# A new opening for a fused graph layer and attention kernel

## The chip, the cores and the metric

The kernel runs on one core of one Trainium2 chip. The metric is the device time of one execution in microseconds; a kernel's time is the median of its runs.

## The reference, cut to what matters

x has 64 elements of 256 nodes by 512 channels (float32), adj is one 256 by 256 graph. Two layers follow each other, both with a residual and a normalization over the channels:

```python
# layer 0
mi = x @ Wi.T;  mj = x @ Wj.T            # W = [Wi, Wj], each 512 x 512
x = layernorm(x + deg[:, None] * (mi + b) + adj @ mj)
# layer 1: masked attention with 8 heads of 64
q, k, v = x @ Wq.T + bq, x @ Wk.T + bk, x @ Wv.T + bv
x = layernorm(x + softmax(mask(q k^T / 8)) v @ Wo.T + bo)
```

## The kernel before, in words

Elements are worked on in 32 groups of two. A tile of x or h has 128 partitions, two row tiles t (nodes) or four column tiles c (channels). The work is written out by hand: nearly every instruction goes through `in_order`, which keeps an engine's instructions in the order of the program text, and the text interleaves the stages of several elements. What isn't passed to `in_order` (in the kernel before, the loads of weights, biases and graph and the stores of factors) is placed by a scheduler.

**Layer 0** (`l0_steps`) computes mi and mj of one element in full fp32 with seven products of blocks instead of eight: sums S1 to S4 of blocks of the transposed x (`sum_x`, `left_steps`) meet combinations T1 to T4 of blocks of the weights. `w0` holds the seven right-hand sides, B11, B21, B22, T1 to T4 (`combine` subtracts one from another). A product is two matmuls of 128x128 by 128x512. Results are put together on VectorE: `u1`, `u2`, `u3` are partial sums, `add_scaled` adds a degree-scaled one to the residual tile `xh`, `mj` is written to SBUF and split into `hi` and `lo`, two fp32r parts that TensorE multiplies at four times the fp32 pace. `neighbours` multiplies both by the graph; `add`, `stat`, `give` finish the layer (residual, statistics with the power on GpSimd, normalization on ScalarE). Before that, `add_bias` on GpSimd adds the degree-scaled bias `degb` to `xh`.

The transposed x comes from `xB`, loaded by `load_xB` in four transfers into one single buffer and turned on VectorE by `turn_x`. `xh` is loaded apart by `load_x`.

**Layer 1** computes q, k, v and the output with three fp32r products each. Left and right sides are split in three parts: `hA`, `hL`, `hD` for h (`split_three`), and head, lift and diff for the weights: one "factor" is a quarter of one of four weight matrices. A step of v, q or k is twelve matmuls. In the first group each of the sixteen factors is made on the chip from the raw weights (`make`) and stored to DRAM (`kept`); later groups load them from there. `bring` fetches or makes the next factor of `queue` into a ring of six buffers (`stream`) and appends it to `coming`, from which the steps (`v_step`, `qk_step`) take theirs.

PSUM has three pools: `ps_m` with three banks (tag mm), `ps_s` with two pairs of banks (tag sc, for scores and some products) and one bank `ps_v`.

**The opening** is the text between the definition of `combine` and the loop over groups: layer 0 of elements 0 and 1, the split of h by transposes on TensorE (`h_transpose`), six factors made at once, then v, q and k of group 0, with the first products of element 2 between k and the scores. All later groups run in the loop.

```python
    run([p[0], p[2], p[3]])
    turn_x(1, "kT")
    ...
    run([p[1], p[4], p[5], q[0], p[6], low0, q[2]])
```

Of the kernel before, what the change touches and what calls it, by code (L numbers as in the profile page):

```python
# [224 lines left out]
def unshifted_path(ctx, tc, flag, x, adj, wiT, wjT, b0, wqT, bq, wkT, bk, wvT, bv, woT, bo, out):  # L225
# [49 lines left out]
    def score_bank(name):  # L275
        return score_banks(name)[:, 0, :]
# [5 lines left out]
    def in_order(ins):  # L282

        tc.keep_in_program_order(ins)
# [7 lines left out]
    def transpose(*args):  # L292
        in_order(nc.tensor.transpose(*args))
# [19 lines left out]
    load_xB(0)  # L313
    w0 = const.tile([P, 7, 2, D], F32, name="w0")
    adj_i = p2.tile([P, NT, N], I32, tag="pe", name="adj_i")
    for n, w, h in ((B11, wiT, 0), (T3, wjT, 0), (None, None, 0), (B21, wiT, 1), (B22, wjT, 1)):
        if n is None:
            nc.sync.dma_start(out=adj_i, in_=adj.rearrange("(t p) j -> p t j", p=P))
        else:
            nc.sync.dma_start(out=w0[:, n], in_=w.rearrange("(p h c) o -> p h c o", h=2, c=2)[:, h])  # L320
    load_x(0)
    nc.sync.dma_start(out=b_bc, in_=b0.to_broadcast([P, D]))

    xT, xS, hP, qT, kT, vv, aoT, aoP = ({} for _ in range(8))

# [21 lines left out]
        in_order(nc.vector.tensor_reduce(deg, a, AX.X, ALU.add))  # L347

    def turn_graph():
        for t in range(NT):  # L350
            pt = score_bank("pt_a")[:, :N]
            for i in range(NT):
                transpose(pt[:, i * P:(i + 1) * P], a[:, i, t * P:(t + 1) * P], ident)

            in_order(nc.vector.tensor_copy(graph[:, t, :], pt))
            in_order(nc.scalar.copy(aT[:, t, :], pt))

    inexact = const.tile([P, 1], F32, name="inexact")

# [7 lines left out]

    def degree_bias():
        for t in range(NT):
            in_order(nc.vector.tensor_scalar(degb[:, t, :], b_bc, deg[:, t:t + 1], None, ALU.mult))  # L370

    def add_bias(b):
        in_order(nc.gpsimd.tensor_tensor(xh[b], xh[b], degb, ALU.add))  # L373
# [1 line left out]

    def load_bias(b, name):
        t = const.tile([P, NC], F32, tag=name, name=name)
        nc.sync.dma_start(out=t, in_=b)
        return t

    def channels(q):

        half, j = divmod(q, 2)
        return slice(j * DH + half * R, j * DH + (half + 1) * R)

    def load_wo(t, c0):
        w = woT.rearrange("(c p) o -> p c o", p=P)
        for q in range(P // R):
            nc.sync.dma_start(out=t[q * R:(q + 1) * R], in_=w[channels(q), c0:c0 + t.shape[1], :])

    bq_sb = load_bias(bq, "bq")
    bk_sb = load_bias(bk, "bk")

    bv_t = const.tile([P, NC], F32, tag="bvt", name="bv_t")
    with nc.allow_non_contiguous_dma(reason="512 numbers, once"):
        for q in range(P // R):
            nc.sync.dma_start(out=bv_t[q * R:(q + 1) * R], in_=bv.rearrange("r (c p) -> p (r c)", p=P)[channels(q)])
    bo_bc = const.tile([P, D], F32, name="bo_bc")
    nc.sync.dma_start(out=bo_bc, in_=bo.to_broadcast([P, D]))
# [6 lines left out]
    def load_raw(name, tiles):  # L406
        n = NC // len(tiles)
        for i, t in enumerate(tiles):
            if name == "wo":
                load_wo(t, n * i)  # L410
            else:
                w = weights[name].rearrange("(p c) o -> p c o", p=P)
                nc.sync.dma_start(out=t, in_=w[:, n * i:n * (i + 1), :])
        raws[name] = tiles

    def raw_tile(tag):
# [14 lines left out]
    queue = []  # L431
    coming = []

    def bring():
        if queue:
            name, j, first = queue.pop(0)
            f = stream.tile([P, 3, D], F32R, tag="factor", name="factor")
            if first:
                make(f, name, j)
            else:  # L440
                in_order(nc.scalar.dma_start(out=f.bitcast(F32), in_=kept[name][j]))
            coming.append(f)

    def make(f, name, j):
        head, lift, diff = (f[:, i, :].rearrange("p (c o) -> p c o", c=NC) for i in range(3))
        low = p3.tile([P, NC, P], F32, tag="lu", name="low")
        for cs, raw in pieces(name, j):
            in_order(nc.scalar.activation(head[:, cs], raw, AF.Identity, scale=DOWN))
            in_order(nc.vector.tensor_sub(low[:, cs], raw, head[:, cs].bitcast(F32)))
            in_order(nc.scalar.activation(lift[:, cs], low[:, cs], AF.Identity, scale=LIFT))  # L450
        in_order(nc.vector.scalar_tensor_tensor(diff, low, LIFT, head.bitcast(F32), ALU.mult, ALU.subtract))
        nc.sync.dma_start(out=kept[name][j], in_=f.bitcast(F32))

    def fold_value_bias():

# [56 lines left out]
    def l0_steps(b):  # L512
# [75 lines left out]
        def give(t):  # L588
# [3 lines left out]
        return ([step1, step2, step3, step4, step5, step6, step7], neighbours, add, stat, give,  # L592
                lambda: lows(0))

    def three(tags):
        return [p1.tile([P, NC, NB * N], F32R, tag=t, name=t) for t in tags]

# [102 lines left out]
    def v_evict(g, i, t, banks):  # L700
        X, Y = banks
        dst = vv[g][:, i, t, :]
        in_order(nc.scalar.activation(dst, X, AF.Identity, scale=UP))
        in_order(nc.vector.tensor_add(dst, Y, dst))

    def v_step(g, i, t, kind, last):
        def run():
            if g not in vv:
                vv[g] = p1.tile([P, NB, NT, D], F32, tag="v", name="v_sb")
            banks = pair(kind)  # L710
            for c in range(NC):
                rows_of_product(banks, hP[g], NT * i + t, coming[0 if last else c], c)
                if last:
                    coming.pop(0)
                    bring()
            v_evict(g, i, t, banks)
        return run

    def v_pair(g, i, kinds, last):
# [238 lines left out]
    combine(T1, T3, B11)  # L958
    degrees()
    combine(T2, B22, T1)  # L960
    combine(T4, B21, T2)
    combine(T3, B22, T3)
    (p, nb0, add0, stat0, give0, low0), (q, nb1, add1, stat1, give1, low1) = l0_steps(0), l0_steps(1)
    run([p[0], p[2], p[3]])
    turn_x(1, "kT")
    load_xB(2)
    degree_bias()
    add_bias(0)
    turn_graph()
    run([p[1], p[4], p[5], q[0], p[6], low0, q[2]])  # L970
    add_bias(1)
    sum_x(1)
    run([q[1], nb0])
    for t in (1, 0):
        add0(t)
        stat0(t)
    give0(1)
    run(q[3:4])
    give0(0)
    h_transpose(0, 1)  # L980
    run(q[4:6])
    h_transpose(0, 0)
    run(q[6:7])
    low1()
    for _ in range(RING):
        bring()
    spread_value_bias()
    v, q_, k = projection_steps(0, "SMSM", False)
    run([v[0], nb1])
    for t in (1, 0):  # L990
        add1(t)
        stat1(t)
    v[1]()
    give1(1)
    h_transpose(1, 1)
    give1(0)
    run(v[3:4])
    h_transpose(1, 0)
    run(v[2:3])
    check_graph()  # L1000
    load_raw("wo", [p1.tile([P, NT, D], F32, tag=t, name="raw") for t in ("mj", "hi")])
    for m in range(NC):
        q_[m]()
        if m < NC - 1:
            k[m]()
        if m == 1:
            turn_x(2)
            load_xB(3)
            add_bias(2)
    load_x(3)  # L1010
    p, q = layer0(1)
    run(p[0][:3])
    sum_x(2)
    turn_x(3)
# [216 lines left out]
```

## Time and profile before

| | us |
|---|---|
| median of 3 runs | 3016.53 (3013.96 to 3017.73) |
| profiled execution, whole | 3014.01 |
| its span, first to last instruction | 3012.2 |
| granted TensorE clock, mean over the span | 0.994 |
| TensorE busy | 2936.1 (97%) |
| VectorE busy | 2327.9 (77%) |
| first matmul of layer 0 starts | 9.31 |
| first scores start | 115.72 |
| a group in the loop | about 93 to 94 |

The profile is of one execution. In its rows an engine is PE (TensorE), PEld (its weight loads), DVE (VectorE), ACT (ScalarE), POOL (GpSimd) or SP (the queue that issues most transfers); L290 is the helper through which all matmuls go, so rows are told apart by the tiles that they write and read (`po<-w,xT`). A name in brackets with an arrow is what ended an engine's idle time before the row. The factors' ring is `factor`; `pxy`, `px` and `py` are the banks of v, q and k.

### The profile page before, as it was taken

How to read it: one execution, taken by the hardware profiler on the slowest of the kernel's cores; microseconds unless marked ns; L12 is line 12 of the kernel's file. 1: busy time of each engine (PE TensorE's matmuls, PEld its weight loads, DVE VectorE, ACT ScalarE, POOL GpSimd, SP SyncE). 2: the span in 40 equal slices, each digit the busy share in tenths (PEclk: the TensorE clock that was granted, in tenths of full speed). 3: DMA queues.
4: the chain of work that ended last, by engine and by line, in shares of the span. 5: the costliest groups of instructions: out<-in, count | busy, mean ns of one | idle time of the engine just before them, and what ended most of it. 6: DMA issues, size and time to landing. Idle time of an engine off the chain costs nothing. (4 is left out here: it accounts for less than half of the span.)

```text
span 3012.2 us, 42600 instructions
## 1 busy us (share of the span) xinstructions
PE 2936.1 (97%) x15638; PEld 1915.1 (64%) x15638; DVE 2327.9 (77%) x3539; ACT 1196.1 (40%) x2247; POOL 1247.8 (41%) x930
## 2 busy tenths in 40 slices
PE   6999999999999999999999999999999999999998
PEld 3566666666666666666666666666666666666655
DVE  6778877778777788776788777887777887777875
ACT  2344344343343343443434443433434434334343
POOL 1144443443443444444444434444344444344443
PEclk8999999999999999999999999999999999999999
DMA  5475556674566655566655566655566555666553
GB/s 197 161 246 190 171 189 229 232 247 148 179 209 230 242 208 170 189 219 226 233 164 191 196 234 238 219 172 182 206 232 238 185 171 198 233 234 216 166 172 133
DMA packets 305605, 609.49 MB, mean 202 GB/s; under 512 B 27632, under 2 KB 189424, under 8 KB 305136
## 3 DMA queue, kind: packets, MB, share of 16 engines
q10 hardware_dynamic: 75808, 391.02, 34.0%
q1 hardware_dynamic: 229584, 215.69, 24.7%
q8 instruction: 126, 2.06, 0.3%
q14 instruction: 87, 0.71, 0.1%
HBM read 494.67 MB, written 78.64 MB: 190 GB/s over the span
## 5 line engine op out<-in xcount | busy, mean ns | idle before, releaser
L831 POOL TENSOR_TENSOR pk<-pe 128x512 f32<-128x512 f32 x256 | 330.5, 1301 | 572.5 <-ACT pe L821 572.5
L290 PE MATMUL po<-w,xS 128*128 128x512 f32 x1024 | 481.7, 603 | 3.5 <-DVE mj L560 2.5
L290 PE MATMUL po<-w,xT 128*128 128x512 f32 x768 | 373.8, 610 | 15.3 <-DVE xS L490 9.3
L472 POOL TENSOR_TENSOR rstd<-ve,mhalf 128x1 f32<-128x1 f32 x256 | 154.1, 602 | 512.5 <-DVE below L470 512.4
L821 ACT ACTIVATE pe<-pe 128x1024 f32<-128x1024 f32 x256 | 270.6, 1057 | 151.7 <-DVE pe L817 151.7
L290 PEld LDWEIGHTS po<-w,xS 128*128 128x128 f32 x1024 | 184.0, 189 | 224.5 <-issue 168.2
L608 POOL TENSOR_TENSOR hL<-hF,hA 128x512 fp32r<-128x512 f32 x93 | 150.9, 1622 | 396.6 <-ACT hA L602 396.6
L817 DVE TENSOR_TENSOR pe<-ps,maskT 128x1024 f32<-128x1024 f32 x256 | 300.9, 1196 | 3.6 <-PE ps L290 3.6
L697 DVE TENSOR_TENSOR kT<-py,kT 128x512 f32<-128x512 f32 x128 | 88.5, 691 | 260.2 <-ACT kT L695 260.2
L373 POOL TENSOR_TENSOR xh<-xh,degb 128x1024 f32<-128x1024 f32 x64 | 152.5, 2382 | 271.8 <-DMA xh<-in_x_dram 107.7
L290 PEld LDWEIGHTS po<-w,xT 128*128 128x128 f32 x768 | 139.1, 191 | 189.5 <-issue 171.7
L290 PE MATMUL ps<-qT,kT 64*128 64x256 f32 x2048 | 256.5, 389 | 0.0
L290 PE MATMUL pav<-pe,v_sb 128*32 128x256 f32 x4096 | 248.7, 382 | 3.5 <-DVE kT L697 1.5
L290 PEld LDWEIGHTS ps<-qT,kT 64*128 64x128 f32 x2048 | 187.0, 186 | 69.3 <-PE pav L290 38.7
L908 DVE RECIPROCAL rden<-den 128x256 f32<-128x256 f32 x127 | 221.9, 1747 | 5.6 <-PE den L290 3.8
L477 ACT ACTIVATE shift<-below,rstd 128x1 f32<-128x1 f32 x256 | 74.4, 291 | 374.0 <-POOL rstd L472 223.3
L290 PEld LDWEIGHTS pav<-pe,v_sb 128*32 128x32 f32 x4096 | 118.4, 109 | 155.2 <-issue 49.2
L478 ACT ACTIVATE xh<-xh,shift,rstd 128x512 f32<-128x512 f32 x256 | 208.8, 816 | 8.8
L859 POOL TENSOR_TENSOR aoT<-aoT,spread 128x512 f32<-128x512 f32 x127 | 205.8, 1621 | 3.4 <-DMA spread<-rden 3.0
L602 ACT ACTIVATE hA<-hF 128x512 fp32r<-128x512 f32 x124 | 77.8, 628 | 296.1 <-DVE hF L496 266.5
L290 PE MATMUL px<-hA,factor 128*128 128x512 f32 x640 | 184.3, 410 | 0.0
L290 PE MATMUL py<-hD,factor 128*128 128x512 f32 x640 | 175.4, 396 | 2.1 <-ACT kT L695 2.1
(133 smaller groups left out, 6053.9 us busy)
## 6 DMA issues: line engine op xcount, KB each, us to landing
factor<-wv ACTq DMA_DIRECT2D x124, 768.0 KB, 6.3
factor<-wq ACTq DMA_DIRECT2D x124, 768.0 KB, 6.6
factor<-wk ACTq DMA_DIRECT2D x124, 768.0 KB, 6.3
factor<-wo ACTq DMA_DIRECT2D x120, 768.0 KB, 7.3
xB<-in_x_dram SPq DMA_DIRECT2D x256, 128.0 KB, 3.5
xh<-in_x_dram SPq DMA_DIRECT2D x64, 512.0 KB, 9.0
h_cols<-xh SPq DMA_DIRECT2D x124, 256.0 KB, 2.3
hB<-h_cols SPq DMA_DIRECT2D x124, 256.0 KB, 3.2
```

Of the source, the lines that this page charges most:

```text
L290: in_order(nc.tensor.matmul(*args, **kw))
L373: in_order(nc.gpsimd.tensor_tensor(xh[b], xh[b], degb, ALU.add))
L472: order(nc.gpsimd.tensor_tensor(rstd, ve, mhalf, ALU.pow))
L478: order(nc.scalar.activation(t, t, AF.Identity, bias=shift, scale=rstd))
L602: in_order(nc.scalar.activation(parts[0], src, AF.Identity, scale=DOWN))
L608: in_order(engine.tensor_tensor(parts[1], src, parts[0].bitcast(F32), ALU.subtract))
L697: in_order(nc.vector.tensor_add(dst, Y, dst))
L817: in_order(nc.vector.tensor_add(pe.rearrange("p j t q -> p j (t q)"), ps.rearrange("p j t q -> p j (t q)"), maskT.rearrange("p t q -> p (t ...
L821: in_order(nc.scalar.activation(flat, flat, AF.Exp, scale=QSCALE, accum_out=etot[:, NB * g + i, pr:pr + 1]))
L831: in_order(nc.gpsimd.tensor_tensor(pk, pe[:, :, 0, :], pe[:, :, 1, :], ALU.add))
L859: in_order(nc.gpsimd.tensor_tensor(d, d, spread, ALU.mult))
L908: in_order(nc.vector.reciprocal(rden, den))
```

## The change

Only the opening and the order of loads are rewritten.

- Layer 0 of elements 0 and 1 uses the new `direct_steps`: eight matmuls for mi and eight for mj, each of 128x128 by 128x512, added up in PSUM. No sums of x and none of the partial sums on VectorE are needed. `mj` stays in PSUM and is split from there. Element 2 and all later ones keep `l0_steps`.
- Three products of element 2 move from behind k to between the steps of v.
- `make` is cut in `begin_make` (head on ScalarE, low on GpSimd instead of VectorE) and `end_makes` (lift on ScalarE, diff on VectorE, store), so several factors can be begun before the first is finished. The first four lows get buffers of their own, in the space of qT; later ones alternate between two (tag hF).
- All loads and stores of the opening go through `in_order`, in a new order: weights of mj before those of mi, the graph and the bias next, the raw weights and later x behind; small loads last.
- The degree bias and the copies of the turned graph move from VectorE to ScalarE.
- Before the first product, 24 matmuls of `ones` by `ones` (128x128 by 128x128) run into the bank of `ps_v`.
- In `qk_step`, also within the loop, `bring` stands after VectorE's addition instead of before it.

The diff, cut to its core:

```diff
-    for n, w, h in ((B11, wiT, 0), (T3, wjT, 0), (None, None, 0), (B21, wiT, 1), (B22, wjT, 1)):
-        if n is None:
-            nc.sync.dma_start(out=adj_i, ...
-    load_x(0)
-    nc.sync.dma_start(out=b_bc, in_=b0.to_broadcast([P, D]))
+    for n, w, h in ((T3, wjT, 0), (B22, wjT, 1), (B11, wiT, 0), (B21, wiT, 1)):
+        in_order(nc.sync.dma_start(out=w0[:, n], ...
...
     def turn_graph():
+        both = score_banks("pt_a")
...
-            in_order(nc.vector.tensor_copy(graph[:, t, :], pt))
-            in_order(nc.scalar.copy(aT[:, t, :], pt))
+        in_order(nc.scalar.copy(graph, both[:, :, :N]))
+        in_order(nc.scalar.copy(aT, both[:, :, :N]))
...
-            in_order(nc.vector.tensor_scalar(degb[:, t, :], b_bc, deg[:, t:t + 1], None, ALU.mult))
+            in_order(nc.scalar.activation(degb[:, t, :], b_bc, AF.Identity, scale=deg[:, t:t + 1]))
...
+    def bring(several=1, left=1):
+        for _ in range(several):
+            if queue:
+                name, j, first = queue.pop(0)
+                f = stream.tile([P, 3, D], F32R, tag="factor", name="factor")
+                coming.append(f)
+                if first:
+                    begin_make(f, name, j)
+                    end_makes(left)
+                else:
+                    end_makes()
+                    in_order(nc.scalar.dma_start(out=f.bitcast(F32), in_=kept[name][j]))
...
+    def begin_make(f, name, j):
+        head, lift, diff = cut(f)
+        low = lows.pop() if lows else p2.tile([P, NC, P], F32, tag="hF", name="low")
         for cs, raw in pieces(name, j):
             in_order(nc.scalar.activation(head[:, cs], raw, AF.Identity, scale=DOWN))
-            in_order(nc.vector.tensor_sub(low[:, cs], raw, head[:, cs].bitcast(F32)))
-            in_order(nc.scalar.activation(lift[:, cs], low[:, cs], AF.Identity, scale=LIFT))
-        in_order(nc.vector.scalar_tensor_tensor(diff, low, LIFT, head.bitcast(F32), ALU.mult, ALU.subtract))
-        nc.sync.dma_start(out=kept[name][j], in_=f.bitcast(F32))
+        for cs, raw in pieces(name, j):
+            in_order(nc.gpsimd.tensor_tensor(low[:, cs], raw, head[:, cs].bitcast(F32), ALU.subtract))
+        started.append((f, low, name, j))
+
+    def end_makes(left=0):
+        while len(started) > left:
+            f, low, name, j = started.pop(0)
+            head, lift, diff = cut(f)
+            in_order(nc.scalar.activation(lift, low, AF.Identity, scale=LIFT))
+            in_order(nc.vector.scalar_tensor_tensor(diff, low, LIFT, head.bitcast(F32), ALU.mult, ALU.subtract))
+            in_order(nc.sync.dma_start(out=kept[name][j], in_=f.bitcast(F32)))
...
+    def direct_steps(b):
...
+        def graph_half(h):
+            if h == 0:
+                k["mj"] = score_banks("po")
+            for t in (1, 0):
+                for c in range(2):
+                    matmul(k["mj"][:, t, :], left(t, h)[:, c, :], w0[:, (T3, B22)[h], c, :],
+                           start=(h == 0 and c == 0), stop=(h == 1 and c == 1))
+
+        def own_half(t):
+            k["mi", t] = bank("po")
+            for h in range(2):
+                for c in range(2):
+                    matmul(k["mi", t], left(t, h)[:, c, :], w0[:, (B11, B21)[h], c, :], ...
+
+        def halves(t):
...
+            in_order(nc.scalar.copy(k["hi"][:, t, :], k["mj"][:, t, :]))
+            in_order(nc.vector.tensor_tensor(k["lo"][:, t, :], k["mj"][:, t, :], k["hi"][:, t, :].bitcast(F32),
+                                             ALU.subtract))
+
+        def add_own(t):
+            r = xh[b][:, t, :]
+            in_order(nc.vector.scalar_tensor_tensor(r, k["mi", t], deg[:, t:t + 1], r, ALU.mult, ALU.add))
...
             in_order(nc.scalar.activation(dst, X, AF.Identity, bias=bias[:, m:m + 1], scale=UP))
+            in_order(nc.vector.tensor_add(dst, Y, dst))
             bring()
-            in_order(nc.vector.tensor_add(dst, Y, dst))
...
+    warm = value_bank("warm")
+    for _ in range(24):
+        matmul(warm[:, :P], ones, ones, start=True, stop=True)
+    in_order(nc.sync.dma_start(out=adj_i, in_=adj.rearrange("(t p) j -> p t j", p=P)))
+    in_order(nc.sync.dma_start(out=b_bc, in_=b0.to_broadcast([P, D])))
     turn_x(0)
+    load_x(0)
     load_xB(1)
     load_x(1)
-    load_x(2)
     load_raw("wv", raw_tile("v"))
+    load_xB(2)
     load_raw("wq", raw_tile("aoT"))
     load_raw("wk", [p5.tile([P, NT, D], F32, tag="xh", name="raw") for _ in range(2)])
-    sum_x(0)
...
+    load_x(2)
+    bq_sb, bk_sb = small_loads()
...
+    mj0(0)
+    mj0(1)
+    halves0(1)
+    halves0(0)
     degrees()
+    mi0(1)
+    turn_graph()
     degree_bias()
     add_bias(0)
     add_bias(1)
+    combine(T1, T3, B11)
+    turn_x(1, "kT")
+    own0(1)
+    mi0(0)
+    nb0()
+    combine(T2, B22, T1)
+    own0(0)
+    add0(1)
+    stat0(1)
     give0(1)
+    add0(0)
+    stat0(0)
     give0(0)
+    combine(T4, B21, T2)
+    mj1(0)
+    mj1(1)
+    bring(3, 9)
+    turn_x(2, "xT")
+    load_xB(3)
+    halves1(1)
+    halves1(0)
+    bring(1, 9)
+    mi1(1)
+    own1(1)
     h_transpose(0, 1)
+    mi1(0)
+    own1(0)
     h_transpose(0, 0)
+    nb1()
+    load_raw("wo", ...
+    end_makes()
+    add_bias(2)
...
+    add1(1)
+    stat1(1)
+    give1(1)
+    add1(0)
+    stat1(0)
+    give1(0)
     v[1]()
+    p[0][0]()
+    v[0]()
+    p[0][2]()
     h_transpose(1, 1)
+    h_transpose(1, 0)
+    p[0][1]()
     run(v[3:4])
+    bring(2)
+    end_makes()
+    combine(T3, B22, T3)
     run(v[2:3])
```

In the last v step, `v_step` calls `bring(2, 9)` once its second column is done and `bring(2)` after its eviction. q and k then alternate, as before, with `sum_x(2)`, `check_graph` and `spread_value_bias` among them; `turn_x(3)` and `load_x(3)` follow, then the first scores.

More of the change, by code (lines that the diff above doesn't have):

```diff
@@ L315, in unshifted_path @@
     adj_i = p2.tile([P, NT, N], I32, tag="pe", name="adj_i")
-    for n, w, h in ((B11, wiT, 0), (T3, wjT, 0), (None, None, 0), (B21, wiT, 1), (B22, wjT, 1)):
-        if n is None:
-            nc.sync.dma_start(out=adj_i, in_=adj.rearrange("(t p) j -> p t j", p=P))
-        else:
-            nc.sync.dma_start(out=w0[:, n], in_=w.rearrange("(p h c) o -> p h c o", h=2, c=2)[:, h])
-    load_x(0)
-    nc.sync.dma_start(out=b_bc, in_=b0.to_broadcast([P, D]))
+    for n, w, h in ((T3, wjT, 0), (B22, wjT, 1), (B11, wiT, 0), (B21, wiT, 1)):
+        in_order(nc.sync.dma_start(out=w0[:, n], in_=w.rearrange("(p h c) o -> p h c o", h=2, c=2)[:, h]))
     xT, xS, hP, qT, kT, vv, aoT, aoP = ({} for _ in range(8))
@@ L349, in turn_graph @@
     def turn_graph():
+        both = score_banks("pt_a")
         for t in range(NT):
-            pt = score_bank("pt_a")[:, :N]
             for i in range(NT):
-                transpose(pt[:, i * P:(i + 1) * P], a[:, i, t * P:(t + 1) * P], ident)
-            in_order(nc.vector.tensor_copy(graph[:, t, :], pt))
-            in_order(nc.scalar.copy(aT[:, t, :], pt))
+                transpose(both[:, t, i * P:(i + 1) * P], a[:, i, t * P:(t + 1) * P], ident)
+        in_order(nc.scalar.copy(graph, both[:, :, :N]))
+        in_order(nc.scalar.copy(aT, both[:, :, :N]))
     inexact = const.tile([P, 1], F32, name="inexact")
@@ L377, in load_bias @@
         t = const.tile([P, NC], F32, tag=name, name=name)
-        nc.sync.dma_start(out=t, in_=b)
+        in_order(nc.sync.dma_start(out=t, in_=b))
         return t
@@ L388, in load_wo, with small_loads @@
         for q in range(P // R):
-            nc.sync.dma_start(out=t[q * R:(q + 1) * R], in_=w[channels(q), c0:c0 + t.shape[1], :])
-    bq_sb = load_bias(bq, "bq")
-    bk_sb = load_bias(bk, "bk")
+            in_order(nc.sync.dma_start(out=t[q * R:(q + 1) * R], in_=w[channels(q), c0:c0 + t.shape[1], :]))
+    def small_loads():
+        with nc.allow_non_contiguous_dma(reason="512 numbers, once"):
+            for q in range(P // R):
+                in_order(nc.sync.dma_start(out=bv_t[q * R:(q + 1) * R],
+                                           in_=bv.rearrange("r (c p) -> p (r c)", p=P)[channels(q)]))
+        in_order(nc.sync.dma_start(out=bo_bc, in_=bo.to_broadcast([P, D])))
+        return load_bias(bq, "bq"), load_bias(bk, "bk")
     bv_t = const.tile([P, NC], F32, tag="bvt", name="bv_t")
-    with nc.allow_non_contiguous_dma(reason="512 numbers, once"):
-        for q in range(P // R):
-            nc.sync.dma_start(out=bv_t[q * R:(q + 1) * R], in_=bv.rearrange("r (c p) -> p (r c)", p=P)[channels(q)])
     bo_bc = const.tile([P, D], F32, name="bo_bc")
-    nc.sync.dma_start(out=bo_bc, in_=bo.to_broadcast([P, D]))
     weights = {"wq": wqT, "wk": wkT, "wv": wvT, "wo": woT}
@@ L412, in load_raw @@
                 w = weights[name].rearrange("(p c) o -> p c o", p=P)
-                nc.sync.dma_start(out=t, in_=w[:, n * i:n * (i + 1), :])
+                in_order(nc.sync.dma_start(out=t, in_=w[:, n * i:n * (i + 1), :]))
         raws[name] = tiles
@@ L432, in unshifted_path @@
     coming = []
[L434 to L446, printed above, removed]
+    started, lows = [], []
@@ L447, in make, with cut @@
+    def cut(f):
+        return [f[:, i, :].rearrange("p (c o) -> p c o", c=NC) for i in range(3)]
+    def begin_make(f, name, j):
+        head, lift, diff = cut(f)
+        low = lows.pop() if lows else p2.tile([P, NC, P], F32, tag="hF", name="low")
         for cs, raw in pieces(name, j):
             in_order(nc.scalar.activation(head[:, cs], raw, AF.Identity, scale=DOWN))
-            in_order(nc.vector.tensor_sub(low[:, cs], raw, head[:, cs].bitcast(F32)))
-            in_order(nc.scalar.activation(lift[:, cs], low[:, cs], AF.Identity, scale=LIFT))
@@ L593, in l0_steps, with left, neighbours, add @@
                 lambda: lows(0))
+    def direct_steps(b):
+        k = {}
+        stats = {}
+        def left(t, h):
+            return xT[b][:, 2 * h:2 * h + 2, t * P:(t + 1) * P]
+        def graph_half(h):
[9 more added lines that the diff above has]
+                for c in range(2):
+                    matmul(k["mi", t], left(t, h)[:, c, :], w0[:, (B11, B21)[h], c, :], start=(h == 0 and c == 0),
+                           stop=(h == 1 and c == 1))
+        def halves(t):
+            if t == 1:
+                k["hi"] = p1.tile([P, NT, D], F32R, tag="hi", name="hi")
+                k["lo"] = p1.tile([P, NT, D], F32R, tag="lo", name="lo")
+            in_order(nc.scalar.copy(k["hi"][:, t, :], k["mj"][:, t, :]))
[4 more added lines that the diff above has]
+            in_order(nc.vector.scalar_tensor_tensor(r, k["mi", t], deg[:, t:t + 1], r, ALU.mult, ALU.add))
+        def neighbours():
+            k["pa"] = score_banks("pa")
+            for n, (part, j) in enumerate((part, j) for part in ("hi", "lo") for j in (1, 0)):
+                for i in (1, 0):
+                    matmul(k["pa"][:, i, :], graph[:, j, i * P:(i + 1) * P], k[part][:, j, :],
+                           start=(n == 0), stop=(n == 2 * NT - 1))
+        def add(t):
+            r = xh[b][:, t, :]
+            in_order(nc.vector.tensor_add(r, k["pa"][:, t, :], r))
+        def stat(t):
+            stats[t] = norm_stats(xh[b][:, t, :], in_order)
+        def give(t):
+            norm_apply(xh[b][:, t, :], *stats[t], in_order)
+        return graph_half, own_half, halves, add_own, neighbours, add, stat, give
     def three(tags):
@@ L714, in run @@
                     coming.pop(0)
-                    bring()
+                    if c == 1:
+                        bring(2, 9)
             v_evict(g, i, t, banks)
+            if last:
+                bring(2)
         return run
@@ L956, in unshifted_path @@
     load_raw("wk", [p5.tile([P, NT, D], F32, tag="xh", name="raw") for _ in range(2)])
-    sum_x(0)
-    combine(T1, T3, B11)
-    degrees()
[L960 to L966, printed above, removed]
+    load_x(2)
+    bq_sb, bk_sb = small_loads()
+    mj0, mi0, halves0, own0, nb0, add0, stat0, give0 = direct_steps(0)
@@ L967, in unshifted_path @@
+    mj1, mi1, halves1, own1, nb1, add1, stat1, give1 = direct_steps(1)
+    spare_lows = p1.tile([P, NC, NC, P], F32, tag="qT", name="lows")
+    lows.extend(spare_lows[:, c] for c in range(NC))
+    mj0(0)
+    mj0(1)
+    halves0(1)
+    halves0(0)
+    degrees()
+    mi0(1)
+    turn_graph()
     degree_bias()
     add_bias(0)
-    turn_graph()
-    run([p[1], p[4], p[5], q[0], p[6], low0, q[2]])
     add_bias(1)
[L972 to L976, printed above, removed]
+    combine(T1, T3, B11)
@@ L977, in unshifted_path @@
+    turn_x(1, "kT")
[6 more added lines that the diff above has]
+    stat0(1)
     give0(1)
-    run(q[3:4])
+    add0(0)
+    stat0(0)
     give0(0)
+    combine(T4, B21, T2)
[9 more added lines that the diff above has]
+    own1(1)
     h_transpose(0, 1)
-    run(q[4:6])
+    mi1(0)
+    own1(0)
     h_transpose(0, 0)
[L983 to L986, printed above, removed]
@@ L987, in unshifted_path @@
-    spread_value_bias()
-    v, q_, k = projection_steps(0, "SMSM", False)
[L989 to L992, printed above, removed]
+    nb1()
+    load_raw("wo", [p1.tile([P, NT, D], F32, tag=t, name="raw") for t in ("mj", "hi")])
+    end_makes()
+    add_bias(2)
+    v, q_, k = projection_steps(0, "SMSM", False)
+    p, q = layer0(1)
+    add1(1)
[4 more added lines that the diff above has]
+    give1(0)
     v[1]()
-    give1(1)
+    p[0][0]()
+    v[0]()
+    p[0][2]()
@@ L995, in unshifted_path @@
     h_transpose(1, 1)
-    give1(0)
+    h_transpose(1, 0)
+    p[0][1]()
     run(v[3:4])
-    h_transpose(1, 0)
+    bring(2)
+    end_makes()
+    combine(T3, B22, T3)
     run(v[2:3])
-    check_graph()
-    load_raw("wo", [p1.tile([P, NT, D], F32, tag=t, name="raw") for t in ("mj", "hi")])
     for m in range(NC):
         q_[m]()
+        if m == 1:
+            sum_x(2)
+        if m == 2:
+            check_graph()
+            spread_value_bias()
         if m < NC - 1:
             k[m]()
[L1006 to L1009, printed above, removed]
+    turn_x(3)
@@ L1010, in unshifted_path @@
     load_x(3)
[L1011 to L1014, printed above, removed]
     run([scores(0, 0), scores(0, 1), p[0][3], k[NC - 1]])
```

## The prediction

> **What bounds the kernel now.** I read the page's shares first, then stretches of the opening, then PE's order of time there.
>
> ```profile
> PE 2936.1 (97%) x15638; PEld 1915.1 (64%) x15638; DVE 2327.9 (77%) x3539; ACT 1196.1 (40%) x2247; POOL 1247.8 (41%) x930
> ...
> PE   6999999999999999999999999999999999999998
> ```
>
> PE is the bound, and its only slack is the first slice (75 us). The steady loop leaves nothing to gain (its groups last 93 to 94 us at 99 to 100% PE), and the change leaves it alone but for one move. So the question is when the loop's work can start. The stretches show it (us; then busy us and instructions of each engine, granted clock, DMA share, GB/s):
>
> ```profile
> 0.00:9.31 9.31, 0.00 (x0) 0.03 (x1) 3.26 (x5) 1.28 (x1) 0.88 (x8) 1.00 0.61 167
> 9.31:28.77 19.46, 12.98 (x28) 5.17 (x29) 11.69 (x16) 1.29 (x3) 2.34 (x1) 1.00 0.85 295
> 28.77:54.90 26.13, 19.28 (x48) 8.97 (x48) 19.13 (x33) 6.78 (x12) 3.61 (x3) 0.93 0.26 72
> 54.90:66.59 11.69, 9.66 (x21) 5.92 (x21) 8.45 (x15) 6.89 (x14) 0.00 (x0) 0.58 0.85 338
> 66.59:83.17 16.58, 12.72 (x46) 9.01 (x44) 9.26 (x21) 5.66 (x11) 3.42 (x3) 0.89 0.37 103
> 83.17:109.52 26.35, 21.69 (x85) 16.89 (x84) 20.94 (x33) 15.37 (x32) 0.00 (x0) 0.90 0.67 261
> 109.52:115.72 6.20, 6.20 (x14) 2.50 (x13) 1.44 (x2) 1.27 (x2) 0.00 (x0) 0.86 1.01 358
> 115.72:134.37 18.65, 18.65 (x62) 9.63 (x61) 13.58 (x15) 3.96 (x7) 9.91 (x5) 1.00 0.40 139
> ```
>
> From 109.52 PE never pauses again. I take the first scores (115.72) as the mark: everything after it is the same in both kernels. Between 9.31 and 115.72 PE is idle for 23.9 us (106.41 less the busy 82.5).
>
> Prices on PE (start, us, what; one fp32 matmul leaves two records, an fp32r one a single record):
>
> ```profile
> 9.31 3.45 PE L290 MATMUL po<-w,xT 128*128 128x512 f32 x4 [9.31 <-DVE xS L490]
> ...
> 20.38 3.60 PE L290 MATMUL po<-w,xS 128*128 128x512 f32 x8
> ...
> 58.33 0.80 PE L290 MATMUL pxy<-factor,hD 128*128 128x512 f32 x1 [0.48 <-DVE factor L451]
> ...
> 83.17 1.07 PE L290 MATMUL pxy<-hA,factor 128*128 128x512 f32 x4
> 84.08 1.07 PE L290 MATMUL pxy<-hD,factor 128*128 128x512 f32 x4
> ```
>
> Eight records in 3.60 us: an fp32 matmul is 0.90, a product of two 1.80. Four fp32r in 0.91: twelve (a v, q or k step) are 2.72. The first product took 3.45 instead of 1.80: half clock. In 54.9 to 66.6 the clock is 0.58 and PE waits at each slice of a factor for VectorE: the weight split, ACT head, DVE low, ACT lift, DVE diff, one factor at a time.
>
> **What the Trainium skill says.** "TensorE: Matmul & The Clock Gate", Part 1: the array idles at half rate and gets the full clock after some 3.4 us of sustained work. The trace agrees: 3.45 us against 1.80. "SBUF — State Buffer", Who interferes with whom: a VectorE instruction with two SBUF inputs contends with a GpSimd one that reads SBUF. The trace agrees, and harshly: a 0.42 us sum took 2.50, ending as GpSimd's add ended.
>
> ```profile
> 37.30 2.50 DVE L489 TENSOR_TENSOR xS<-xS,xT 128x256 f32<-128x256 f32 x1
> ```
> ```profile
> 37.01 2.51 POOL L373 TENSOR_TENSOR xh<-xh,degb 128x1024 f32<-128x1024 f32 x1 [9.08 <-DVE xh L530]
> ```
>
> **Removed, added, moved.** Work on PE up to the mark, at full clock, before: 14 products of elements 0 and 1, 25.2; three of element 2, 5.4; two neighbour sums of eight fp32r, 4.0; five sets of transposes, 2.9; four v steps, 10.9; seven q/k steps, 19.0. Sum 67.4. Add the first wait of 9.3 and 39.0 remain: 23.9 idle, 15.1 half clock and its like. After: 32 direct matmuls of 0.90 are 28.8 instead of 25.2, so 71.0. The change pays 3.6 us of matmul to shorten the chains.
>
> *VectorE* loses, for two elements, eight sums of x (3.4), four u and four mj sums (5.5), four of eight scaled adds (3.0), sixteen factors' lows (11.7), degree bias and graph copy (1.6): about 25 us of the 74 busy before the mark. That gain is worth only what PE waits for.
>
> *Start.* 24 products of ones run from about 1.2 us (ones is written at 0.92 + 0.20). At a quarter of 0.90 each warm and twice that cold they end near 9 (4 us cold are nine, fifteen more take 3.4). No row shows them; weight loads (0.19) could make them 0.38 each: then 12. I take 9.5. x is turned at 8.06 as before. The first weight needed, T3, now leaves first at 3.48, and the first landed after 5.7: 9.2. PE starts at 9.5 at full clock, worth 1.65.
>
> *SP's queue.* At most eight transfers are under way: bk leaves at 9.28 as the first weight lands, bv at 11.81 as the second does (4.13 + 7.7). Bytes came at some 230 GB/s until 10 us and 400 after, with about 2.2 us to landing. In the new order that gives T3 9.2, B22 11.6, B11 13.1, B21 14.4, adj 15.1, b_bc 15.7, x(0) 17.0. xB(1), before behind bq, bk, four bv and bo (17.20), now waits only for turn_x(0) and free places: four issues from 8.5 to 13.1, landing about 18. x(1) lands at 20, wv at 22. xB(2) blocks SP until turn_x(1) has read xB(1), 22.4; wq, wk, x(2) and the small loads stand behind it and land by 35; they are needed from 40 on (x(2)) and 61 (wq). xB(3) blocks until turn_x(2), near 37; the wo loads and stores behind it are not due before 44. All free under PE.
>
> *PE's chain* from 9.5: mj of element 0 until 16.7 (weights 11.6: in time), mi until 20.3, graph 20.9, mi 24.5, neighbours 26.5. ACT's graph copies (0.6 each) end at 22.2, so nb0 isn't late. ACT's degree bias 23.7 (0.6 to 0.8 each, between the factor row, 0.62, and the norm row, 0.81), GpSimd's bias adds 26.1 and 28.5 (2.4 each): VectorE stands 3.5 us at own0(1), behind it T2, own0(0), the adds and stats, T4, turn_x(2). T2 reads two SBUF operands and is held to 28.5 by the second bias add. Row 0 is normalized at 35.7, row 1 at 33.9; PE asks for them at 41.5 and 37.3. Cover left: 3 to 5 us. xT(1) is ready at 22.4, asked for at 26.5. So element 1 runs to 44.1 without a pause.
>
> Then stalls, each by the rows: v[1] waits for the first diff (VectorE is free of h's splits at 44.1, 0.69 each) and follows four of them: 1.5. p[0][2]'s add frees p[0][1]'s bank and h's split frees v[3]'s: 1.2. Factors 4 to 9: ACT heads after v[3]'s eviction, GpSimd's low (1.3 to 1.6: pk and hL rows), then lift; factor 4's diff is held by GpSimd's next low: 1.1. ACT serves two more heads and three lifts before q0's and k0's evictions, so k1's second bank comes 1.8 late. Sum 5.6. From q2 ACT has about 4.3 us for each pair against PE's 5.4.
>
> Mark: 9.5 + 71.0 + 5.6 = 86.1 against 115.72: **29.6 us less**. The moved refill in qk_step stays in ACT's same place for the loop: nothing. The profiled execution (3014.01, span 3012.2) becomes 2984.4. The median of the runs shown lies 2.5 above it, so 2984.4 to 2986.9; I take 2985.5.
>
> **Rivals.** *A, 20 to 24 us gained: the hand-over to GpSimd binds.* For: the 2.50 us row. If each of factors 4 to 11 costs low 1.62 plus diff 0.69 in turn, with ACT behind, eight take 18.5; they start at 62, and the q/k steps then lose another 4 to 7. Against: 2.3 a factor is under PE's 2.72. About 2992.
> *B, 20 to 26 gained: PE goes cold again* between 44 and 62, among small gaps, or the ones end at 12 or leave the clock low. Price: up to 12 us at half rate is 6, or 1.7 at the start, or 2.5. Against: no gap over 2 us in my chain; the cold spell before followed 2.4 idle and sparse work. About 2990.
> *C, slower: the moved refill.* In each of 31 groups eight q/k steps now ask for their next factor after VectorE's add (0.69) is issued. Should that hold back the transfer, 248 steps lose up to 0.69, 171 us, so 3155; from 0.12 a step the opening's gain is gone. Against: add and transfer stand on different queues, ACT's order is unchanged, and six buffers lie between.
> *D, no change:* the loop takes the gain back, a transfer or buffer being due at a fixed time. PE at 100% from 109.5 speaks against it: it has no wait to grow.
>
> **Numbers.** Forecast 0.68, A 0.14, B 0.13, C 0.03, D 0.02. Forecast's own range: no stalls and a start at 9.2 give 2978; stalls doubled with the median's 2.5 give 2992.5. With A and B the range is 2977 to 2997. About 0.2% (6 us) is what a measurement can tell from no change. Faster 0.95, same 0.02, slower 0.03.
>
> **What would show it.** Right: the first four po records in about 1.8 us near 9.5; clock near 1.00 in every ten us to 86; pauses of PE totalling 4 to 7 us between; the first ps row at 83 to 89; low rows on POOL at 1.3 to 1.6. A shows as POOL lows over 2 us or diffs of 1.5 and more, with PE idle before px or py; B as a clock under 0.8; C as PE waiting for the factor's transfer in every group. The forecast is wrong if the first scores come near 86 and the span hasn't shrunk by as much, or if they come after 98.

## The result, and the profile after

The changed kernel takes 2984.03 us (median of 5 runs, 2979.46 to 2985.37) against 3016.53 (3012.09 to 3017.73): the ratio is 0.9892, 95% interval 0.9877 to 0.9906, so 28 to 37 us less. Its profiled execution took 2979.46 us with a span of 2977.2.

The shares of the page, and PE's row of forty slices:

```profile
PE 2934.5 (99%) x15694; PEld 1917.7 (64%) x15694; DVE 2310.1 (78%) x3497; ACT 1194.6 (40%) x2243; POOL 1273.0 (43%) x950
...
PE   9999999999999999999999999999999999999998
```

PE's busy sum has hardly moved (2936.1 to 2934.5, of which the ones now are 8.2); the first slice, once a 6, is full. The stretches of the opening, cut at the start of the first product, of v, of q and of the first scores (us; then busy us and count of PE, PEld, DVE, ACT, POOL; clock, DMA share, GB/s):

```profile
0.00:9.36 9.36, 8.18 (x48) 8.19 (x49) 2.11 (x1) 1.28 (x1) 0.88 (x8) 1.00 0.64 209
9.36:42.74 33.38, 32.80 (x94) 16.44 (x93) 20.78 (x29) 10.98 (x21) 13.49 (x9) 1.00 0.84 248
42.74:63.17 20.43, 18.13 (x69) 12.08 (x68) 12.35 (x24) 7.52 (x15) 3.08 (x5) 1.00 0.48 182
63.17:86.78 23.61, 21.50 (x86) 16.50 (x84) 21.14 (x24) 16.26 (x31) 16.79 (x15) 0.93 0.79 320
86.78:105.44 18.66, 18.66 (x62) 9.62 (x61) 14.22 (x16) 5.16 (x9) 9.92 (x5) 1.00 0.82 272
```

The first scores start at 86.78 instead of 115.72, and the first values follow 18.66 us behind (18.65 before). From the first product to v PE is busy for 32.80 of 33.38 us, where it was for 32.26 of 45.59. v with element 2's three products takes 20.43; before, v took 28.27 and the products another 6.20 behind q and k. q and k take 23.61 instead of 26.35. The differences, 12.2, 14.0 and 2.7, make up the 28.9 at the mark. (The neighbour sum of element 1 stood behind v's first step before and now stands ahead of v, so the first two differences are not of quite the same work.)

PE's order of time has six pauses up to the mark, 5.0 us together: 0.58, 0.86, 0.81, 0.64, 0.20 and this one (start, us, what, the pause and who ended it):

```profile
1.18 8.35 PE L290 MATMUL warm<-ones 128*128 128x128 f32 x48 [1.18 <-POOL ones L327]
9.36 10.46 PE L290 MATMUL po<-w,xT 128*128 128x512 f32 x24
...
74.82 1.78 PE L290 MATMUL py<-hD,factor 128*128 128x512 f32 x4 [1.91 <-ACT kT L758]
76.40 1.91 PE L290 MATMUL px<-hL,factor 128*128 128x512 f32 x4
```

The ones last until 9.5 and the first twelve fp32 matmuls run at 0.87 each. The last two rows are k's second step: after a pause of 1.91 us for ScalarE, which holds the bank, eight matmuls take 3.29 us instead of 1.82, at half clock.

### The profile page after: what moved, and what is told of

It reads as the page before. It is cut to its first block, busy times and chain, and to the rows that moved or that the text cites. A ratio compares the mean times of both kernels' runs of the same rounds, so it can differ in the third digit from the quotient of the medians.

```text
span 2977.2 us, 42690 instructions
## 1 busy us (share of the span) xinstructions
PE 2934.5 (99%) x15694; PEld 1917.7 (64%) x15694; DVE 2310.1 (78%) x3497; ACT 1194.6 (40%) x2243; POOL 1273.0 (43%) x950
## 5 line engine op out<-in xcount | busy, mean ns | idle before, releaser
L290 PE MATMUL po<-w,xS 128*128 128x512 f32 x992 | 466.1, 602 | 1.5 <-DVE mj L570 1.5
L290 PE MATMUL po<-w,xT 128*128 128x512 f32 x808 | 387.4, 604 | 0.8 <-ACT u L549 0.8
L290 PEld LDWEIGHTS po<-w,xS 128*128 128x128 f32 x992 | 177.8, 189 | 214.6 <-issue 162.2
L290 PEld LDWEIGHTS po<-w,xT 128*128 128x128 f32 x808 | 145.6, 189 | 180.5 <-issue 179.0
```

What stands on the lines that cost most here:

```text
L290: in_order(nc.tensor.matmul(*args, **kw))
```

## The experiments

Marks of every profile, in us from the span's start. "Net" is first scores less first product, as the start of the first product varies: it comes when x and its weight have landed and, where there are ones, when these have ended.

| kernel | first po | v | q | first scores | net | first values |
|---|---|---|---|---|---|---|
| before | 9.31 | 54.90 | 83.17 | 115.72 | 106.41 | 134.37 |
| changed | 9.36 | 42.74 | 63.17 | 86.78 | 77.42 | 105.44 |
| no ones | 8.57 | 44.36 | 64.76 | 86.79 | 78.22 | 106.12 |
| old split, new text | 8.33 | 52.28 | 70.61 | 100.22 | 91.89 | 118.88 |
| old text, new split | 8.71 | 55.87 | 84.14 | 108.97 | 100.26 | 127.66 |
| lows on VectorE | 9.29 | 49.53 | 68.51 | 87.86 | 78.57 | 106.78 |
| small loads first | 9.30 | 42.68 | 63.11 | 86.73 | 77.43 | 105.39 |
| k's bank | 9.12 | 42.59 | 62.95 | 83.79 | 74.67 | 104.33 |
| evictions earlier | 9.18 | 41.71 | 60.72 | 81.55 | 72.37 | 102.07 |
| mixed lows | 8.22 | 40.85 | 59.84 | 79.16 | 70.94 | 98.15 |
| changed, again | 9.50 | 42.88 | 63.32 | 86.91 | 77.41 | 105.58 |

The kernels that were executed once took, in the table's order, 2986.20, 2996.32, 3003.04, 2976.73, 2986.52 and 2994.12 us. These times don't follow the marks (k's bank is 3 us earlier at the scores than the changed kernel and 10 slower): from the first values to the end the profiles take 2868 to 2888 us, by chance in the loop (last section). So the marks are compared.

**No ones.**

```diff
-    warm = value_bank("warm")
-    for _ in range(24):
-        matmul(warm[:, :P], ones, ones, start=True, stop=True)
```

> The changed kernel without the 24 matmuls of ones. My theory (PE is the bound from 9.4 us to the first scores, so a slower start moves everything behind it): the first po product takes about 3.4 us for its first four records instead of 1.8, and the first scores come 1.6 to 2.2 us later, at 88.4 to 89.0 instead of 86.8. Rival (PE's opening has slack, the chain is VectorE's): the first scores stay within 0.5 us of 86.8.

The scores didn't move (86.79), but not for the rival's reason: v starts 1.62 later although the first product starts 0.79 earlier, so the cold start costs 2.4 from there on. PE is the bound there. The loss came back at k's second step:

```profile
76.41 1.20 PE L290 MATMUL py<-hD,factor 128*128 128x512 f32 x4 [1.90 <-ACT kT L758]
77.44 1.07 PE L290 MATMUL px<-hL,factor 128*128 128x512 f32 x4
```

The same pause of 1.90 us, and this time no half clock behind it. So my theory held up to q and failed at the mark, by a thing that it had not: whether the clock falls behind a pause depends on where in time the pause lies (last section).

**The split as before, in the new text.**

```diff
                 if first:
-                    begin_make(f, name, j)
-                    end_makes(left)
+                    make(f, name, j)
```

> The changed kernel with the split of each weight factor made as before (head, low on VectorE, lift, diff, one factor after the other) at the places where the new text begins a factor. My theory (direct products and staged split each carry part, and each needs the other): VectorE gets some 7 us between element 1's products and its splits, v starts about 9 us later and q/k lose 3 more, first scores at 96 to 101. Rival 1 (the direct products made nearly all of the gain): 90 or less. Rival 2 (the split made nearly all of it): 108 or more.

First scores 100.22, within my range, outside both rivals'. PE's pauses, but for one of 0.62 (start, us, what, pause):

```profile
47.97 1.10 PE L293 MATMUL pt_h<-ident,xh 128*128 128x128 f32 x4 [9.25 <-DVE xh L646]
...
79.47 1.78 PE L290 MATMUL pxy<-hA,factor 128*128 128x512 f32 x4 [3.26 <-DVE v_sb L776]
86.30 1.19 PE L290 MATMUL py<-hD,factor 128*128 128x512 f32 x4 [1.29 <-ACT kT L767]
98.17 1.20 PE L290 MATMUL py<-hD,factor 128*128 128x512 f32 x4 [2.99 <-ACT kT L767]
```

Four factors, made one after the other, stand on VectorE ahead of element 1's own add: 9.25 us of PE in one piece.

**The new split in the old text.** `bring`, `begin_make`, `end_makes`, four lows of their own, the refills in v's last step and behind the addition of q and k as in the changed kernel, and

```diff
-    for _ in range(RING):
-        bring()
...
+    bring(NC, 9)
+    end_makes()
+    bring(2)
+    end_makes()
```

> The kernel before, with only the staged split over three engines put in (own lows for the first four, two buffers for the later ones, addition before refill in q and k). My theory: v, q and k gain 4 to 8 us, layer 0 nothing, first scores at 108 to 112 instead of 115.7. Rival (the split made most of the gain): 102 or less. Rival (GpSimd's lows hold VectorE's diffs so that nothing is gained): 115 or more.

First scores 108.97, in the range: 6.7 us gained. All the rest of the change (direct products, order, loads, ones; the run before this one) gained 15.5. Together they gain 28.9, 6.7 more than their sum. Each is one profile, and openings of the kernel before differ by 3 us (end of this section), which puts these 6.7 between 4.4 and 7.5. My reading, which no run tests: with the split staged, the factors are begun while PE is busy with element 1, and this cover exists only in the new order. Nor does a run have the new order with seven products, so what the direct products bring by themselves stays open.

**The lows on VectorE.**

```diff
-            in_order(nc.gpsimd.tensor_tensor(low[:, cs], raw, head[:, cs].bitcast(F32), ALU.subtract))
+            in_order(nc.vector.tensor_tensor(low[:, cs], raw, head[:, cs].bitcast(F32), ALU.subtract))
...
             if last:
+                end_makes(1)
                 bring(2)
```

> The changed kernel with the lows on VectorE instead of GpSimd (and one factor finished before the eighth and ninth are begun). My theory: VectorE has no idle time between 33 and 46 us, so the first four lows (0.69 each) and their wait for the heads put v off by about 3 us; later the diffs are no longer held by GpSimd, which gives back up to 3 in q/k: first scores at 87 to 90, diffs at 0.69 each instead of up to 1.7. Rival (moving the lows off VectorE is the core of the gain): 95 or more. Rival (the shared ports cost more than GpSimd brings): under 86.5.

87.86 at the mark, in the range, but from two terms larger than mine: v is 6.8 us late (I said 3), q to scores takes 19.35 instead of 23.61. The early loss is one pause of PE and half clock behind it:

```profile
45.22 1.10 PE L293 MATMUL pt_h<-ident,xh 128*128 128x128 f32 x4 [5.54 <-DVE xh L637]
```

The late gain is VectorE no longer held. The diffs of the later twelve factors, first in the changed kernel, then in this one (busy us, mean ns | idle before):

```profile
L461 DVE SCALAR_TENSOR_TENSOR factor<-low,factor 128x512 fp32r<-128x512 f32 x12 | 13.4, 1120 | 3.0 <-POOL low L453 3.0
```

```profile
L461 DVE SCALAR_TENSOR_TENSOR factor<-low,factor 128x512 fp32r<-128x512 f32 x12 | 8.1, 682 | 0.0
```

Twelve times 0.44 us are 5.3 us in which a diff stood behind a GpSimd low. So GpSimd is right for the first four lows and wrong for the other twelve.

**Small loads first.**

```diff
     load_x(0)
+    bq_sb, bk_sb = small_loads()
     load_xB(1)
...
-    bq_sb, bk_sb = small_loads()
```

> The changed kernel with the small loads (bv in four, bo, bq, bk) issued before xB(1), as in the kernel before. My theory (the load order is mostly cover): xB(1) lands near 23 us instead of 18, the turned x(1) is there near 25, just when PE asks for it (25.4): first scores at 86.8 to 88. Rival (the order of loads brought a good part of the gain): 91 or more.

No difference at all (86.73). The four issues of xB(1) leave at 15.9 to 18.4 instead of 8.0 to 11.4, and x(1) is still turned at 21.12 (21.18 in the changed kernel), when VectorE has come to it. That part of the load order is cover.

**k's bank.**

```diff
-                ... (kT, "kT", bk_sb, "MMMA")))
+                ... (kT, "kT", bk_sb, "MMMA" if paired else "MAMA")))
```

> The changed kernel with k's second step in group 0 taking its second bank from the idle value bank instead of the three shared ones, where it waits 1.9 us for ScalarE to free one and PE then runs 3.4 us at half clock. My theory: both go, first scores at 83.0 to 84.0. Rival (ScalarE's backlog of splits is the bound and only moves to the next step): 85.5 or more.

83.79, as expected, the half clock gone as well. But the first values came only 1.1 us earlier, as two new pauses stood up, the second behind the mark:

```profile
81.75 1.20 PE L290 MATMUL py<-hD,factor 128*128 128x512 f32 x4 [0.89 <-ACT kT L758]
87.59 1.98 PE L290 MATMUL po<-w,xS 128*128 128x512 f32 x4 [1.80 <-DVE kT L759]
```

The rival's point was right one step later: the backlog of splits moved on, from ScalarE to VectorE.

**Evictions earlier.** Besides the bank: `halves1` ahead of `give0(0)`, T4 and `turn_x(2)`; `v[1]` ahead of `give1(1)`; `add_bias(2)` behind `give1(0)`.

> The bank of the run before, and besides: hi and lo of element 1 before the fourth normalization and before T4 and the turn of x(2); v[1]'s eviction before the normalizations of element 1; element 2's bias add behind them. My theory: the pauses before pt_h (0.6), at v[1]'s first diff (0.9), and before p[0][2] (0.8) go for the greater part, first scores at 81.0 to 82.5, PE's work alone giving 80.4; time 4 to 6 us under the changed kernel, if the loop has as many late transfers. Rival: VectorE's chain is only shifted and the scores stay at 83 to 84.

81.55 at the mark, in the range; the pauses before pt_h and p[0][2] are gone, the one in v[1] is 0.52. The pause of 1.80 behind the mark stays, so the first values come 3.4 us earlier and not 5.2. The median of four runs is 2981.51 (2975.83 to 2984.67), ratio on record 0.9876 (0.9859 to 0.9892) to the kernel before (the medians give 0.9885): not distinct from the changed kernel, where 4 to 6 us were expected.

**Mixed lows, and the changed kernel again**, on the same chip. To the edits of the run before come `end_makes(1)` ahead of the last v step's `bring(2)` and

```diff
+        engine = nc.gpsimd if lows else nc.vector
         low = lows.pop() if lows else p2.tile([P, NC, P], F32, tag="hF", name="low")
...
+            in_order(engine.tensor_tensor(low[:, cs], raw, head[:, cs].bitcast(F32), ALU.subtract))
```

> The improved opening (bank of k's second step, hi and lo of element 1 earlier, v[1]'s eviction earlier) with the lows of the first four factors on GpSimd and those of the later twelve on VectorE, the eighth and ninth begun after the seventh is ended. Theory (before q GpSimd brings 5.3 us, in q and k it costs 4.3): v at 41.7, q at 60.7, q and k at PE's own 19.0 to 19.5, first scores at 79.7 to 80.5, first values at 98.5 to 99.5; 4 to 9 us under the changed kernel's median in the same call. Rival (VectorE, with the graph check and the sums of x among q and k, becomes late): first scores at 82 or more, or the first values over 20 us behind them.

The scores come at 79.16, half a us ahead of the range, as the ones ended at 8.16 here and not near 9.5. That is 70.94 behind the first product; the values come 18.99 later. From first product to scores (columns as above):

```profile
8.22:79.16 70.94, 69.78 (x244) 44.28 (x244) 53.16 (x90) 34.80 (x66) 14.38 (x11) 1.00 0.80 275
```

PE rests for 1.2 us in all. The median is 2976.78 (four runs, 2967.93 to 2981.34) beside 2982.65 (2978.56 to 2984.01) for the changed kernel and 3015.73 for the one before, ratio to the latter on record 0.9879 (0.9860 to 0.9898; the medians give 0.9871). The profiles say 6.5 us net less than the changed kernel, the medians 5.9; the runs of the two overlap, so that it beats the changed kernel is likely, not shown.

> The changed kernel once more, against the kernel before on the same chip. The opening alone is worth 28.9 us in the profiles. Theory (the loop is the same, and what differs there is how many groups meet late transfers): medians 26 to 33 us apart, 28.9 within the interval, first scores again near 86.8. Rival (the loop gained too, some 4 us by the moved refill or the earlier start): 33 or more, with a typical group shorter than 90.67.

The ratio is 0.9890 (0.9873 to 0.9908). The medians are 33.1 us apart, the openings of the first two profiles 28.9. Over all runs up to then the means lay 32.9 apart. For the rival a typical group should have become shorter; the shortest are 90.66, 90.66 and 90.67 (before, changed, again) and the medians 90.8, 90.9 and 91.1. So the kernel before was profiled three times more.

> The kernel before, profiled again. Over all runs so far its mean lies 32.9 us above the changed kernel's, 4 more than the openings of the two profiles are apart. Theory 1 (its opening varies, by where its pauses meet half-clock windows): first scores at 117 to 122. Theory 2 (chance in the loop): first scores within 1 us of 115.7 and 2870 to 2888 us from the first values to the end, as in the ten profiles of changed kernels (mean 2875.7). Theory 3 (its loop is longer by 4): 2880 on average over three such profiles.

Its first scores came at 117.98, 117.37 (repeat 2) and 114.89 (repeat 3); first values to the end took 2875.5, 2874.8 and 2877.5, beside 2877.85 in the first profile and 2875.7 on average in ten profiles of changed kernels. Theory 3 falls. Theory 1 holds in part: the old opening varies by 3 us, the new one (86.78, 86.91) hardly. The half-clock windows are there: from its first rise to the mark the clock is at half for 27.3 us in the two late openings (it rises first at 18.24 and 14.02), for 23.9 us in the other two (12.33 and 11.53). Four old openings average 116.5, so the gain at the mark is 29.6. What is left of the 32.9, some 3 us, is within the loop's scatter, and no run assigns it.

## Why the prediction was right

2985.5 was forecast, 2984.03 measured, the way and most steps as argued. Point by point:

- *PE is the bound, and the start of the loop moves everything.* Right: 28.94 at the scores and 28.93 at the first values.
- *Work of 71.0 us on PE.* 1.2 too high: the mixed kernel, at full clock throughout, was busy for 69.78 of the 70.94 us from first product to scores. That the 3.6 us of matmul paid for shorter chains were worth it fits, but no run parts them from the new order.
- *Start at 9.5.* 9.36, at full clock. The ones set it: they end at 9.5, as forecast, while the first weight landed at 7.9 (4.4 after its issue at 3.48) and not at 9.2, and x was turned at 8.0. So here they held the first product for 1.4 us; a shorter row wasn't tried. How long they last differs, as they run at half clock until 6.9 here and until 4.1 in the mixed kernel, where they end at 8.16. The Trainium skill ("TensorE: Matmul & The Clock Gate", Part 1) has the gate open after some 3.4 us of work; here it took 5.7 us from the first of the ones, in the mixed kernel 2.9. Without the ones the start costs 2.4 (I said 1.65).
- *SP's queue hidden.* Right: no pause of PE between 9.4 us and the mark was ended by a transfer, and delaying xB(1) by 7 us changed nothing.
- *Element 1 without a pause.* One pause of 0.58: element 1's own add held the bank of pt_h, as VectorE had stood 1.56 us for a hi that was queued behind three factor heads on ScalarE. T2's hold was there: 2.70 us instead of 1.22. VectorE's busy time up to the mark fell by 17.8 us (74.2 to 56.4), not by 25: such holds took part of it back.
- *Stalls of 5.6.* 5.0 in pauses, placed a little otherwise: v[1] 0.86 (1.5 forecast), p[0][2] and v[3] 0.81 and 0.64 (1.2), q0 0.20 (1.1), k's second step 1.91 (1.8). Missing from my sum was the half clock behind the last: 3.42 us at half, which is 1.7 lost. Sum: 9.36 + 69.8 + 5.0 + 1.7 = 85.9, against 86.78; by difference the other 0.9 lie in slower matmuls beside the pauses. So 86.1 came that near because a work sum 1.2 too high stood in for the half clock: that part is luck.
- *Rival A.* Its mechanism was real, its size not: lows took 1.37 us (eight of 128x512), no more than forecast, but the diffs were held for 5.3 us in all. Its signs were there too: two diffs of 1.74 and 1.75 us, and PE idle before py. The Trainium skill ("SBUF — State Buffer", Who interferes with whom) has a VectorE instruction with two SBUF inputs contend with a GpSimd one that reads SBUF; the 1120 ns a diff beside GpSimd's lows, 682 without, agree. With the lows on VectorE q to scores is 4.3 us shorter, which holds the 1.91 and the half clock; my forecast had 1.8 and 1.1 of it.
- *Rival B* came as one half-clock stretch of 3.4 us. *C and D* fell: the shortest groups last 90.66 before and after.
- *The loop.* "Its only slack is the first slice", "PE never pauses again" and groups of 93 to 94 us were misread: a usual group lasts 90.7, and of PE's 76 us of idle time before, 43 lie behind the mark, in a few long groups and at the end. The changed kernel has 36.5 there, so this left the argument whole.
- *The number.* The opening was forecast at 29.6 and gave 28.9 in the two profiles, 29.6 over four old openings. The medians lie 32.5 apart, the first two profiles 34.6. That 2984.03 lies within 1.5 us of 2985.5 is in part chance: the median's offset, taken from the first profile, and some 3 us of the gain come from the loop's scatter.

## What to carry to other kernels

Where one engine is full in the loop, an opening is worth what that engine doesn't do in it: add up its work at full rate, add the first wait, and look at who ends each pause. Buying shorter chains with more of the bound engine's own work can pay when the chains have made it idle for longer (here 3.6 us of work against 23.9 idle). Work handed to a helper engine is free only while the first engine isn't at two-input work of its own: hand it over where there is cover, and keep it where there is none. A pause of the bound engine that looks short, some 2 us, can cost nearly as much again through the clock.

## What the runs showed of the hardware

A pause of PE of 1.9 us was followed by 3.4 us at half clock in three profiles (the changed kernel twice, and with the small loads first) and not in the one without the ones. The traces show why. In each of the fourteen, the changes of the clock lie whole multiples of 3.413 us apart, to within 0.001: time falls into equal steps, and where these lie differs between executions. Below are two such steps of the changed kernel, then three of the kernel without the ones (columns as before; the clock is third from the end):

```profile
71.77:75.18 3.41, 1.50 (x8) 0.92 (x7) 2.78 (x3) 2.70 (x6) 2.97 (x3) 1.00 0.88 359
75.18:78.60 3.42, 3.42 (x10) 2.65 (x9) 3.39 (x5) 2.70 (x6) 3.12 (x3) 0.50 1.02 414
```

```profile
71.31:74.72 3.41, 3.20 (x15) 2.31 (x13) 3.07 (x3) 2.97 (x6) 2.72 (x4) 1.00 0.77 315
74.72:78.14 3.42, 1.73 (x8) 1.43 (x9) 2.99 (x3) 2.99 (x7) 2.73 (x4) 1.00 1.00 401
78.14:81.55 3.41, 3.41 (x17) 2.83 (x16) 3.34 (x5) 2.97 (x6) 2.71 (x3) 1.00 1.03 416
```

In the changed kernel the pause lies whole in one step (PE is busy for 1.50 of 3.41 us), and the clock is at half for the next. Without the ones a border at 74.72 cuts the pause into 0.21 and 1.69, and the clock stays. Over all steps at full clock of the fourteen traces, the clock fell after each in which PE was idle for more than 2.02 us and after none with less than 1.81; in between both occur. So such a pause costs 1.7 us more or nothing, by where it lies.

In each profile four to six groups of the loop (from the first `pav` matmul of one to that of the next) last over 92.5 us, up to 98.4, instead of 90.7, in every kernel. In those over 95 us h's way through DRAM is late: two reads of h take 6.2 to 8.5 us to land, where 3.3 is usual. Here are the transfers of a usual stretch of the kernel before, then of one in a long group (KB each, median us to landing).

```profile
h_cols<-xh SPq DMA_DIRECT2D x2, 256.0 KB, 2.3
hB<-h_cols SPq DMA_DIRECT2D x2, 256.0 KB, 4.0
```

```profile
h_cols<-xh SPq DMA_DIRECT2D x2, 256.0 KB, 3.7
hB<-h_cols SPq DMA_DIRECT2D x2, 256.0 KB, 8.0
```

VectorE then stands 5.39 us before it can turn h, its adds come late, and PE waits 3.10 us for one of them:

```profile
731.06 1.15 DVE L496 STREAM_TRANSPOSE hF<-hB 128x512 f32<-128x512 f32 x1 [5.39 <-DMA hB<-h_cols]
...
735.67 0.51 PE L290 MATMUL pxy<-factor,hA 128*128 128x512 f32 x1 [3.10 <-DVE xh L749]
```

Why the transfers are late wasn't tried; in some groups of usual length reads of h take up to 7.1 us as well. These groups make most of the scatter between executions. From the first values to the end the fourteen profiles take 2867.9 to 2887.6 us; without what the groups over 92.5 take beyond 90.66, 2849.7 to 2856.0.
